# Last two heads' output products by token halves, with half of the routed layer's norm inside the attention's list schedule

## The chip, the cores and the metric

The kernel runs on one core of one Trainium2 chip. The metric is the device time of one execution in microseconds (us), the median of several runs. Positions in the text, such as "at 1092.9", are us from the start of the profiled execution's span.

## The reference, cut to what matters

512 tokens (4 sequences of 128) of width 2048 go through three residual layers: a small attention with a gated MLP, a 4-bit attention, and a routed layer. The change touches the end of the second and the beginning of the third.

```python
# 4-bit attention, added to x
w = (qw.astype(float32) - 8) * repeat(scales, 128, axis=0)     # _dequant_matmul: x @ w
q, k, v = (dequant_matmul(layernorm(x), w) for w in (q, k, v)) # 32 heads, 8 key heads, 128 wide
ctx = softmax(rope(q) @ rope(k).T / sqrt(128) + causal) @ v    # within each sequence
x = x + dequant_matmul(ctx, qw_o, scales_o)                    # the output product
# routed layer, added to x
h = layernorm(x)                                               # over the 2048 features of a token
base = h @ base_w.T + base_b
comb = top-2 of softmax(h @ router_w.T), normalised            # 16 experts
x = x + base + 0.5 * einsum(comb, h @ A.T, B)
```

The layer norm of a token needs all 2048 features of that token, so it can start only when every head's output product for that token has been added. It needs nothing of the other tokens.

## The kernel before

The residual x lives in SBUF as `R`, 16 feature tiles of 128 partitions by 512 tokens. The normed input of a layer lives as a pair `Nh`, `Nl` (a high and a low part, both in the reduced fp32r format of TensorE).

**The 4-bit attention.** There are 48 projections `u` (for each of 8 groups: key, value, 4 queries), each of 16 blocks, and 32 output products `h`, each of 16 blocks. A block (`Stream.block`, L1596) is two matmuls, high part (L1605) and low part (L1606), into a PSUM bank of 512 columns with tag `u` (6 of them), and an eviction that multiplies by the block's scale and adds. The eviction has two forms: `take_d` (L1614), one VectorE instruction that adds to `R` in place, or `take_p`, a ScalarE copy with a scale (L1624) followed by a GpSimd addition (L1628). The 4-bit weights come as int32 in three DMAs a head (`Stream.load`, L1581; 4 buffers `wi`), and ScalarE converts them (L1585; 6 buffers `wq`). Between projection and output product stands `attend` (L1719): scores (L1727, L1729), a maximum on VectorE (L1733), four exponentials and four divisions on ScalarE (L1739, L1750), a transpose (L1755), a copy (L1759), the product with the values (L1764), and the split of the result into `oh` (ScalarE, L1768) and `ol` (VectorE, L1771). These use two PSUM banks with tag `a`.

**What sets the order.** This whole stage is a list schedule: `op(engine, kind, emit, rank, needs, takes, gives)` records an operation, and `Plan.run` (L235) plays all engines through with the times of `Plan.TIME`. Whenever an engine is free it takes the ready operation with the lowest rank whose buffer (`takes`) has room, and emits it. The instruction order of TensorE, VectorE, ScalarE and GpSimd is then fixed as emitted, and on the chip each engine works through its list in order. Projection `u` has ranks from about `u` to `u + 1.8`. The output product of head `h`, which is query `i` of group `g` with `u = 6g + 2 + i`, has ranks from `u + 4.3 + 0.5 i`, over 1.5. For head 31 that is 52.8 to 54.3, and for head 30 it is 51.3 to 52.8. The choice between `take_d` and `take_p` is made in `Plan.run` by which engine comes free sooner.

**The routed layer** is recorded by another planner, `Deferred`, and ordered by `Deferred.solve` (L487): rank is the place in the program minus a shift from the table `RANKS`. It begins with the norm, one sequence `b` at a time: `Norm.enter(b)` transposes `R` back to tokens by features (4 PSUM tiles of 4 transposes each), takes statistics on VectorE, a root on GpSimd, and scales three tiles on ScalarE and one on VectorE. `Norm.leave(b)` transposes back (16 transposes) and splits into `Nh` (ScalarE) and `Nl` (VectorE). In program order: enter 0, 1; leave 0, 1; enter 2, 3; `low(halves[0])`, the router's and A's product for the first 256 tokens; the base product of two feature tiles for these tokens; leave 2, 3; and so on. All its instructions show as L485, the helper that issues them. Its SBUF and PSUM pools are opened after those of the attention are closed, so its tiles lie where the attention's did. The weights for `low` and for the first half of base tile 0 (`first_w`) are loaded and split during the attention.

Of the kernel before, what the change touches and what calls it, by code (L numbers as in the profile page):

```python
# [23 lines left out]
P = 128  # L24
B, S = 4, 128
T = B * S
# [35 lines left out]
K0 = 2  # L62
EARLY, EARLY_D = 2, ((1, 2), (1, 4), (1, 5), (1, 7))
# [3 lines left out]
    "add_x6": -277, "add_x7": -367, "add_x8": -331, "add_x9": -323, "base0": 108, "base11": -220, "base12": 23,  # L67
    "base13": -477, "base14": 9, "base15": -96, "base16": 1, "base19": -5, "base2": -665, "base20": -64,
    "base22": 17, "base23": -26, "base24": -125, "base25": 45, "base26": 70, "base27": -436, "base28": 53,
    "base30": -225, "base31": -44, "base32": -3, "base34": 73, "base35": -163, "base4": 30, "base5": -455,  # L70
    "base6": 382, "base7": 131, "base8": 18, "base9": 30, "bn0": 447, "bn1": -286, "bn2": -65, "bn3": 123,
    "bn3_0": 172, "bn3_1": 24, "bn3_10": 16, "bn3_11": 8, "bn3_12": 26, "bn3_13": -9, "bn3_14": -5,
    "bn3_15": 10, "bn3_16": -26, "bn3_17": 65, "bn3_18": -473, "bn3_2": 80, "bn3_20": -38, "bn3_21": -229,
    "bn3_22": 31, "bn3_24": -14, "bn3_25": -9, "bn3_26": -60, "bn3_27": 33, "bn3_28": -94, "bn3_29": -26,
    "bn3_3": 19, "bn3_30": 3, "bn3_31": -12, "bn3_4": 122, "bn3_5": 44, "bn3_6": 166, "bn3_7": -66,
# [14 lines left out]
    "enter3_2": 27, "enter3_3": -448, "enter3_4": 1213, "enter3_5": 351, "enter3_6": 130, "enter3_7": 10,  # L90
    "enter4": -529, "enter5": -21, "enter6": -1, "enter8": -294, "enter9": -89, "finish0": 27, "finish11": -18,
    "finish12": -195, "finish15": -89, "finish3": -1, "finish4": -155, "finish5": -15, "finish6": -50,
    "finish7": -9, "finish8": 59, "finish9": -55, "gated0": 78, "gated1": -102, "gated10": 12, "gated11": 104,
    "gated12": -23, "gated13": 24, "gated14": -122, "gated15": 58, "gated16": 133, "gated17": 34, "gated18": 20,
    "gated19": 28, "gated2": 91, "gated20": 123, "gated21": 89, "gated22": 12, "gated23": 69, "gated24": -1,
    "gated25": 2, "gated26": 65, "gated27": -130, "gated28": -215, "gated29": 8, "gated3": -2576, "gated30": 37,
    "gated31": -244, "gated4": 14, "gated5": -11, "gated6": 11, "gated7": -387, "gated8": -12, "gated9": -38,
    "load_ctx0": 117, "load_ctx1": 1, "load_ctx10": 86, "load_ctx11": -315, "load_ctx12": 65, "load_ctx13": 82,
    "load_ctx15": -2, "load_ctx2": 188, "load_ctx3": 12, "load_ctx4": -124, "load_ctx5": 100, "load_ctx6": -142,
    "load_ctx7": 77, "load_ctx8": 36, "load_ctx9": -136, "load_od0": -210, "load_od1": -129, "load_od10": 37,  # L100
    "load_od11": 265, "load_od12": 230, "load_od13": -71, "load_od14": -376, "load_od15": 55, "load_od2": 310,
    "load_od3": -29, "load_od4": 144, "load_od5": 102, "load_od6": -3, "load_od7": -1075, "load_od8": 201,
    "load_od9": -35, "low0": 196, "low1": 169, "low10": 0, "low11": 8, "low12": -96, "low13": -16, "low14": 58,
    "low15": -43, "low2": -38, "low3": -191, "low3_0": -226, "low3_1": -103, "low4": -12, "low5": -243,
    "low6": -68, "low7": 25, "low8": 333, "low9": -49, "mix0": 184, "mix1": 68, "mix10": 36, "mix11": 40,
    "mix12": 436, "mix13": 37, "mix14": -678, "mix15": -4, "mix2": 177, "mix3": 117, "mix4": -213, "mix5": 170,
    "mix6": 195, "mix7": 104, "mix8": -107, "norm0": 567, "norm1": 890, "norm2": 861, "norm3": -2, "out0": -4,
    "out1": 43, "out2": -47, "out3": 90, "out_a0": -344, "out_a1": 133, "out_a2": 14, "out_a3": 8,
    "out_m0": -47, "out_m1": -193, "out_m10": -332, "out_m11": 138, "out_m12": 108, "out_m13": -908,
    "out_m14": -492, "out_m15": -264, "out_m2": 156, "out_m3": -122, "out_m4": -698, "out_m5": 6, "out_m6": 163,  # L110
    "out_m7": -70, "out_m8": -90, "out_m9": -162, "outer0": -203, "outer1": -4, "outer2": -226, "outer3": -108,
    "parts0": 40, "parts1": -22, "parts10": -390, "parts11": 82, "parts12": -109, "parts13": -475,
    "parts14": 58, "parts15": -549, "parts16": -213, "parts17": -28, "parts18": 3, "parts19": -1, "parts2": 54,
    "parts20": 124, "parts21": 110, "parts22": -46, "parts23": 106, "parts24": 110, "parts25": -157,
    "parts26": 148, "parts27": 191, "parts29": 129, "parts3": -21, "parts30": 67, "parts31": 24,
    "parts32": -100, "parts33": 109, "parts34": -11, "parts35": 422, "parts36": 135, "parts37": 158,
    "parts38": 231, "parts39": 152, "parts4": -1166, "parts40": -50, "parts41": -111, "parts42": 71,
    "parts43": 47, "parts44": 78, "parts45": 165, "parts46": -30, "parts47": -332, "parts48": 39, "parts49": 7,
    "parts5": -71, "parts50": 63, "parts51": 7, "parts52": -361, "parts53": -25, "parts54": 40, "parts55": 23,
    "parts56": 56, "parts57": -275, "parts58": 124, "parts59": 107, "parts6": 79, "parts60": -87, "parts61": 49,  # L120
    "parts62": 95, "parts63": 6, "parts64": 8, "parts65": 122, "parts66": -9, "parts67": 26, "parts68": -195,
    "parts69": -6, "parts7": 66, "parts70": 122, "parts71": 138, "parts72": -68, "parts8": -22, "parts9": -45,
    "pick0": -72, "product0": -3, "product1": 22, "product10": 17, "product11": -86, "product2": -7,
    "product3": 83, "product4": 72, "product5": 79, "product6": 56, "product7": 14, "product8": -71,
    "product9": -73, "rate0": 1, "rate1": 11, "rate2": 47, "rate3": 62, "rate4": 89, "rate5": -41, "rate6": 9,
    "rate7": -8, "root0": -54, "root1": 647, "root2": 37, "root2_0": 54, "root2_1": 97, "root2_2": 110,
    "root2_3": 180, "root2_4": 84, "root2_5": -74, "root2_6": 215, "root2_7": 79, "root2_8": -6,
    "root2_9": -291, "root3": 529, "root3_0": 16, "root3_1": 3, "root3_2": 171, "root3_3": -42, "root3_4": 293,
    "root3_5": 9, "rope0": -66, "rope1": -145, "rope2": -211, "rope3": -180, "rope4": 68, "rope5": 48,
    "rope6": -33, "rope7": -20, "route0": -78, "rows0": -15, "rows1": 103, "rows2": 129, "rows3": 59,  # L130
    "rows_a0": -25, "rows_a1": 125, "scores0": -314, "scores1": 133, "scores2": 7, "scores3": 165, "select0": 7,
    "select1": -13, "select2": 44, "select3": -1101, "select4": -80, "select5": -380, "select6": -709,
    "select7": -620, "silu0": -55, "silu1": -20, "silu10": -56, "silu11": -14, "silu12": 40, "silu13": 35,
    "silu14": 91, "silu15": 78, "silu2": -69, "silu3": 4, "silu4": 144, "silu5": 123, "silu6": 157,
    "silu7": 113, "silu8": 162, "silu9": 219, "soft0": 41, "soft1": 76, "soft10": 37, "soft11": 80,
    "soft12": 44, "soft13": 179, "soft14": 163, "soft15": 52, "soft2": 158, "soft3": 83, "soft4": 77,
    "soft5": 164, "soft6": 131, "soft7": 87, "soft8": 141, "soft9": 130, "split0": -29, "split1": -478,
    "split10": -19, "split11": -260, "split12": -267, "split13": -301, "split14": -894, "split15": -914,
    "split16": -92, "split17": 29, "split18": -105, "split19": -485, "split2": -74, "split3": -10,
    "split3_0": -208, "split3_1": 29, "split3_10": -8, "split3_11": 13, "split3_14": 11, "split3_15": 70,  # L140
    "split3_16": 12, "split3_17": 55, "split3_18": 1, "split3_19": -10, "split3_2": 93, "split3_20": 201,
    "split3_22": -8, "split3_23": -12, "split3_24": 116, "split3_25": 41, "split3_26": 28, "split3_27": 21,
    "split3_29": 3, "split3_3": -15, "split3_30": 2, "split3_31": -2, "split3_32": 6, "split3_33": 15,
    "split3_34": 210, "split3_35": 32, "split3_36": -2, "split3_37": 6, "split3_38": 116, "split3_39": -20,
    "split3_40": -18, "split3_41": -54, "split3_5": -1, "split3_6": -29, "split3_7": 48, "split3_8": 13,
# [1984 lines left out]
```

## Time and profile before

| what | us |
|---|---|
| median of 3 runs (1413.06 to 1416.96) | 1414.34 |
| the profiled execution | 1413.73 |
| its span | 1411.9 |
| TensorE busy in the span | 1349.8 |
| VectorE / ScalarE / GpSimd busy | 1069.2 / 892.2 / 851.3 |
| last matmul of the attention starts | 1103.20 |
| GpSimd's last addition to `R` ends | 1105.82 |
| first matmul of the routed layer's base product starts | 1118.27 |
| last wait of the chain: VectorE's output instruction starts | 1408.00 |

The span is the time between the first and the last record; the execution is 1.8 us longer. TensorE is the busiest engine by far, at 96% of the span. Matmuls are pipelined, so a matmul's own record (0.39 us for 512 columns) is longer than the distance from one to the next (0.23 us), and the distance is what counts for the time.

### The profile page before, as it was taken

The numbers are of one execution on the slowest core, as the hardware profiler recorded it, in microseconds if no ns is written. First come the engines' busy times: TensorE is split into PE (matmuls) and PEld (weight loads), VectorE is DVE, ScalarE is ACT, GpSimd is POOL, SyncE is SP. The second block draws the span as 40 slices with busy tenths as digits, with TensorE's granted clock in tenths as the row PEclk, the third lists the DMA queues.
The fourth block names the chain that finished last, engine by engine and source line by source line (L and its number), as shares of the span: only waits on it lengthen the run. The fifth ranks groups of instructions, "written<-read, shape, count | busy, mean of one in ns | idle before, by whom it ended". The sixth has DMA issues, their size and how long they took to land.

```text
span 1411.9 us, 21943 instructions
## 1 busy us (share of the span) xinstructions
PE 1349.8 (96%) x7604; PEld 1144.6 (81%) x7604; DVE 1069.2 (76%) x1615; ACT 892.2 (63%) x1734; POOL 851.3 (60%) x700
## 2 busy tenths in 40 slices
PE   4999899999979999999999999999999899999998
PEld 4967898899966888888888888888887798888887
DVE  6886995797978999999999999999998734322221
ACT  5867555556776878878888787888888532211120
POOL 7782253262368798998989999898999302000000
PEclk9999999999999999999999999999999899999999
DMA  6120014655536354444444444444442112433331
GB/s 217 46 68 1 1 61 147 186 169 171 180 116 181 110 156 129 135 141 143 145 134 145 137 141 146 133 142 138 129 142 92 60 60 75 149 105 111 113 105 45
DMA packets 66983, 169.64 MB, mean 120 GB/s; under 512 B 9656, under 2 KB 11832, under 8 KB 66872
## 3 DMA queue, kind: packets, MB, share of 16 engines
q1 hardware_dynamic: 66872, 168.24, 38.2%
q8 instruction: 60, 0.98, 0.3%
q14 instruction: 51, 0.42, 0.1%
HBM read 153.53 MB, written 4.19 MB: 112 GB/s over the span
## 4 chain that ended last, share of the span: by engine, by line
PE 70%; DMA 4%; DVE 4%; ACT 3%; POOL 2%; issue 1%; SPq 0%; ACTq 0%; DVEq 0%; POOLq 0%
PE ps_q L485 21%; PE ps_u L1605 20%; PE ps_u L1606 19%; PE ps_p L485 4%; PE ps_a L1764 2%; PE ps_a L1729 2%; DMA st<-in_w_ctx 2%; DVE W L485 1%; DMA wi<-in_w_h 1%; PE ps_a L1755 1%; ACT W L485 1%; POOL acc L1628 1%; DMA st<-in_w_od_m 1%; DMA st<-in_xf 1%; PE acc L485 1%
## 5 line engine op out<-in xcount | busy, mean ns | idle before, releaser
L1614 DVE SCALAR_TENSOR_TENSOR acc<-ps_u,s_h,acc 128x512 f32<-128x512 f32 x506 | 376.9, 746 | 29.8 <-PE ps_u L1606 4.2
L1605 PE MATMUL ps_u<-Nh,wq 128*128 128x512 f32 (+1 forms) x768 | 305.5, 399 | 5.9 <-ACT wq L1585 2.6
L1606 PE MATMUL ps_u<-Nl,wq 128*128 128x512 f32 (+1 forms) x768 | 299.5, 391 | 0.0
L1628 POOL TENSOR_TENSOR R<-R,scaled 128x512 f32<-128x512 f32 x195 | 253.2, 1308 | 25.5 <-ACT scaled L1624 24.8
L1628 POOL TENSOR_TENSOR acc<-acc,scaled 128x512 f32<-128x512 f32 x184 | 240.1, 1305 | 27.6 <-ACT scaled L1624 26.0
L1614 DVE SCALAR_TENSOR_TENSOR R<-ps_u,s_o,R 128x512 f32<-128x512 f32 x317 | 230.6, 745 | 18.7 <-PE ps_u L1606 14.8
L1605 PE MATMUL ps_u<-oh,wq 128*128 128x512 f32 x512 | 209.0, 408 | 1.1 <-ACT oh L1768 0.7
L1606 PE MATMUL ps_u<-ol,wq 128*128 128x512 f32 x512 | 203.3, 397 | 0.9 <-DVE ol L1771 0.9
L1585 ACT ACTIVATE wq<-wi 128x640 fp32r<-128x640 int32 (+1 forms) x240 | 184.6, 770 | 23.2 <-PE ps_u L1606 18.8
L1605 PEld LDWEIGHTS ps_u<-Nh,wq 128*128 128x128 f32 x768 | 145.0, 189 | 46.3 <-ACT scaled L1624 8.5
L1606 PEld LDWEIGHTS ps_u<-Nl,wq 128*128 128x128 f32 x768 | 145.2, 189 | 30.3
L1624 ACT ACTIVATE scaled<-ps_u,s_o 128x512 f32<-128x512 f32 x195 | 132.8, 687 | 50.6 <-PE ps_u L1606 39.9
L485 ACT CAST w3h<-w 128x1024 fp32r<-128x1024 f32 x47 | 49.4, 1052 | 174.3 <-PE ps_q L485 152.6
L485 DVE TENSOR_TENSOR w3l<-w,w3h 128x1024 fp32r<-128x1024 f32 x47 | 57.5, 1223 | 122.6 <-ACT w3h L485 121.6
L1624 ACT ACTIVATE scaled<-ps_u,s_h 128x512 f32<-128x512 f32 (+1 forms) x188 | 127.2, 678 | 18.4 <-PE ps_u L1606 16.2
L1605 PEld LDWEIGHTS ps_u<-oh,wq 128*128 128x128 f32 x512 | 97.5, 190 | 25.6 <-ACT scaled L1624 3.5
L1606 PEld LDWEIGHTS ps_u<-ol,wq 128*128 128x128 f32 x512 | 97.4, 190 | 21.3 <-DVE ol L1771 1.7
L485 PE MATMUL ps_q<-Nh,w3l 128*128 128x512 f32 (+1 forms) x272 | 102.5, 377 | 0.0
L485 PE MATMUL ps_q<-Nh,w3h 128*128 128x512 f32 (+1 forms) x272 | 102.2, 376 | 0.0
L485 PE MATMUL ps_q<-Nl,w3h 128*128 128x512 f32 (+1 forms) x272 | 102.1, 375 | 0.0
L485 PE MATMUL ps_p<-Y,W 128*128 128x256 f32 x768 | 97.2, 285 | 2.2 <-DVE W L485 1.7
L485 PEld LDWEIGHTS ps_p<-Y,W 128*128 128x128 f32 x768 | 93.6, 191 | 3.4 <-DVE W L485 2.4
(251 smaller groups left out, 2654.4 us busy)
## 6 DMA issues: line engine op xcount, KB each, us to landing
wi<-in_w_h SPq DMA_DIRECT2D x96, 320.0 KB, 3.4
wi<-in_w_o SPq DMA_DIRECT2D x64, 320.0 KB, 3.5
wi<-in_w_h SPq DMA_DIRECT2D x48, 384.0 KB, 3.2
st<-in_w_ctx SPq DMA_DIRECT2D x32, 512.0 KB, 3.6
w<-in_w_base SPq DMA_DIRECT2D x32, 512.0 KB, 3.5
wi<-in_w_o SPq DMA_DIRECT2D x32, 384.0 KB, 3.3
swap<-acc SPq DMA_DIRECT2D x78, 128.0 KB, 2.6
st<-in_w_od_m SPq DMA_DIRECT2D x16, 512.0 KB, 3.7
```

The lines of the kernel that those rows point to most:

```text
L485: getattr(getattr(self.nc, c.engine), c.name)(*c.args, **c.kwargs)
L1585: nc.scalar.activation(w[:, : n * P], box["wi"][:, : n * P], AF.Copy, bias=-8.0)
L1605: nc.tensor.matmul(pm, self.w[i], hi, start=True, stop=False)
L1606: nc.tensor.matmul(pm, self.w[i], lo, start=False, stop=True)
L1614: "v", "less" if part else "evict", lambda: nc.vector.scalar_tensor_tensor(acc(), box["pm"], s, acc(), ALU.mult, ALU.add),
L1624: nc.scalar.activation(t, box["pm"], AF.Copy, scale=s)
L1628: "g", part + "add", lambda: nc.gpsimd.tensor_tensor(acc(), acc(), box["t"], ALU.add),
L1729: nc.tensor.matmul(sc[:, bs], q[:, bs], k[:, bs], start=False, stop=(b == B - 1))
L1755: nc.tensor.transpose(tp[:, bs], box["s"][:, bs], ident)
L1764: nc.tensor.matmul(po[:, bs], vals[h // HEADS][:, bs], box["pt"][:, bs], start=True, stop=True)
```

## The change

For the last two heads (`HALVED = 2`: 30 and 31) the output product is issued in two halves of 256 tokens. The first halves keep their ranks. The second halves get ranks 56 and 56.5, and their weights are loaded and converted a second time; in the list schedule these loads wait for the end of head 31's attention (`after`). The norm of sequences 0 and 1 moves from the routed layer into the list schedule as `normed(b, ...)` with ranks 50 and 51, ready when the first halves of all heads are in `R` (`r_half[0]`). It takes its PSUM tiles from the attention's tags (two `a` and two `u` a sequence) and its SBUF tiles from the attention's `acc`, `qT` and `swap`. The routed layer then starts with enter 2, enter 3. Some 90 entries of `RANKS` are changed too; all are steps of the routed layer (names such as `base`, `bn3_16` and up, `split3_`, `finish`), and the numbering of `bn3_`, `enter3_`, `root3_` and `turn4_` there now starts at sequence 2.

```diff
+HALVED = 2
...
-        "values": (0.89, 1.1), "half": (0.233, 0.43), "less_v": (0.39, 0.58), ...
+        "values": (0.89, 1.1), "half": (0.233, 0.43), "pow": (0.7, 0.85), "less_v": (0.39, 0.58), ...
...
-            def __init__(self, src, order, rank, step):
+            def __init__(self, src, order, rank, step, after=()):
+                self.after = list(after)
...
-                got = op("S", "dma", load, rank - DMA_LEAD, takes="wi")
+                got = op("S", "dma", load, rank - DMA_LEAD, self.after, takes="wi")
...
-        def output(h, rank, ready):
-            st = Stream(io["w_o"][h], range(KT), rank, OUT_SPAN / KT)
+        def output(h, rank, ready, cols=ALL, after=()):
+            st = Stream(io["w_o"][h], range(KT), rank, OUT_SPAN / KT, after)
+            ends = r_last if cols == ALL else r_half[cols.start]
             for m in range(KT):
-                acc = lambda m=m: R[:, m, :]
+                acc = lambda m=m: R[:, m, cols]
                 s = s_o[:, h * KT + m : h * KT + m + 1]
-                how = take(acc, s)
+                before = [o for o in {id(o): o for o in (ends[m], r_last[m])}.values() if o]
                 last = st.block(
-                    m, rank + OUT_SPAN * (m + 0.5) / KT, lambda h=h: outs[h], [ready], how,
-                    [r_last[m]] if r_last[m] else [],
+                    m, rank + OUT_SPAN * (m + 0.5) / KT, lambda h=h: tuple(a[:, cols] for a in outs[h]), [ready],
+                    take(acc, s, "" if cols == ALL else "less"), before[:1], cols,
                 )
-                r_last[m] = last
-            plan.ops[plan.last_block].gives.append("oh")
+                ends[m] = last
+            if cols.stop == T:
+                plan.ops[plan.last_block].gives.append("oh")
+
+        r_half = {c: [None] * KT for c in (0, T // 2)}
+
+        def normed(b, rank, ready):
+            bs = slice(b * S, (b + 1) * S)
+            box, tok, z = {}, {}, {}
+            banks, places = ("a", "a", "u", "u"), (("acc", "acc", "acc", "swap"), ("qT", "qT", "qT", "swap"))[b]
+            def turn(t):
+                tok[t] = tp = (ps_a if banks[t] == "a" else ps_u)()
+                for c in range(C):
+                    nc.tensor.transpose(tp[:, c * P : (c + 1) * P], R[:, 4 * c + t, bs], ident)
+            def stat(t):
+                if t == 0:
+                    box["st"] = tiny.tile([P, HT, 6], F32, tag="stats", name="stats")
+                nc.vector.bn_stats(box["st"][:, t, :], tok[t])
+            def mean():
+                box["mv"] = mv = tiny.tile([P, 2], F32, tag="mv", name="mv")
+                nc.vector.bn_aggr(mv, box["st"].rearrange("p t s -> p (t s)"))
+            def root():
+                box["rs"] = rstd(tiny, box["mv"][:, 1:2])
+            def shift():
+                box["nm"] = nm = tiny.tile([P, 1], F32, tag="nmr", name="nmr")
+                nc.vector.scalar_tensor_tensor(nm, box["mv"][:, 0:1], -1.0, box["rs"], ALU.mult, ALU.mult)
+            def scale(t):
+                z[t] = tmp(places[t])
+                if t in ZD:
+                    nc.vector.tensor_scalar(z[t], tok[t], box["rs"], box["nm"], ALU.mult, ALU.add)
+                else:
+                    nc.scalar.activation(z[t], tok[t], AF.Identity, scale=box["rs"], bias=box["nm"])
+            def back(q):
+                tok[q] = tp = (ps_a if banks[q] == "a" else ps_u)()
+                for i in range(4):
+                    nc.tensor.transpose(tp[:, i * P : (i + 1) * P], z[i][:, q * P : (q + 1) * P], ident)
+            def high(q):
+                nc.scalar.copy(Nh[:, 4 * q : 4 * q + 4, bs], heads(tok[q]))
+            def low(q):
+                d = (slice(None), slice(4 * q, 4 * q + 4), bs)
+                nc.vector.tensor_tensor(Nl[d], heads(tok[q]), Nh[d].bitcast(F32), ALU.subtract)
+            last = None
+            for t in range(HT):
+                p = op("p", "turn", lambda t=t: turn(t), rank, ready, takes=banks[t])
+                last = op("v", "reduce", lambda t=t: stat(t), rank, [p] + ([last] if last else []))
+            last = op("v", "root", mean, rank, [last])
+            last = op("g", "pow", root, rank, [last])
+            last = op("v", "root", shift, rank, [last])
+            ups = [
+                op("v" if t in ZD else "s", "evict", lambda t=t: scale(t), rank, [last], takes=places[t], gives=[banks[t]])
+                for t in range(HT)
+            ]
+            for q in range(HT):
+                p = op(
+                    "p", "turn", lambda q=q: back(q), rank, ups, takes=banks[q],
+                    gives=list(places) if q == HT - 1 else [],
+                )
+                h = op("s", "copy", lambda q=q: high(q), rank, [p])
+                op("v", "low", lambda q=q: low(q), rank, [h], gives=[banks[q]])
...
-                output(h, u + OUT_AT + 0.5 * i, ready)
+                output(h, u + OUT_AT + 0.5 * i, ready, ALL if h < NH - HALVED else slice(0, T // 2))
                 done[h] = ready
+        for b in range(2):
+            normed(b, NU + 2.0 + b, r_half[0])
+        for h in range(NH - HALVED, NH):
+            output(h, NU + 8.0 + 0.5 * (h - NH + HALVED), done[h], slice(T // 2, T), [done[NH - 1]])
...
-        for b in (0, 1):
-            norm.enter(b)
-        for b in (0, 1):
-            norm.leave(b)
         for b in (2, 3):
             norm.enter(b)
         low(halves[0])
```

## Prediction, made before the changed kernel was run

> **What bounds the kernel now.** I read the table of stages around the seam first, in steps of 6 us. Columns: stage, its length, then busy us of PE, PEld, DVE, ACT and POOL, the granted clock, DMA share, GB/s.
>
> ```profile
> 1078.00:1084.00 6.00, 5.08 (x31) 4.25 (x30) 6.00 (x9) 4.73 (x10) 5.48 (x5) 1.00 0.18 64
> 1084.00:1090.00 6.00, 5.53 (x25) 4.15 (x23) 5.51 (x10) 5.21 (x15) 6.00 (x6) 1.00 0.00 0
> 1090.00:1096.00 6.00, 4.58 (x16) 3.29 (x17) 1.44 (x2) 1.81 (x4) 2.13 (x2) 0.70 0.01 3
> 1096.00:1102.00 6.00, 6.00 (x21) 4.81 (x20) 3.58 (x5) 2.82 (x5) 5.00 (x4) 0.73 0.00 0
> 1102.00:1108.00 6.00, 5.16 (x39) 4.44 (x38) 4.29 (x8) 1.38 (x2) 4.02 (x5) 1.00 0.18 61
> 1108.00:1114.00 6.00, 2.49 (x17) 2.17 (x16) 5.15 (x13) 3.52 (x6) 1.56 (x4) 0.91 0.29 115
> 1114.00:1120.00 6.00, 6.00 (x41) 5.59 (x40) 5.26 (x10) 4.76 (x9) 0.00 (x0) 0.81 0.00 0
> ```
>
> Before 1090 four engines are nearly full. Then the clock falls to 0.70 and 0.73, and from 1108 to 1114 PE has 2.49 us of work in 6. The chain of waits says why (start, us, what):
>
> ```profile
> 1090.44 0.59 ACT softT L1759
> 1091.08 1.17 PE ps_a L1764 x8
> 1092.27 0.59 ACT oh L1768
> 1092.91 0.80 PE ps_u L1605
> ...
> 1105.86 3.09 DVE stats L485 x5
> ...
> 1110.48 1.45 ACT scaled L485 x2
> 1111.97 296.00 PE ps_q L485 x1475
> ```
>
> Head 31's softmax ends the first gap, the norm's chain (statistics, root, scale) the second, and from 1112 on PE is the chain to the end. So any us that PE starts its steady work earlier is a us of the span. The timeline of PE gives the two ends:
>
> ```profile
> 1104.42 3.71 PE L485 MATMUL ps_q<-ident,R 128*128 128x128 f32 x32 [0.84 <-ACT scaled L1624]
> 1111.31 0.33 PE L485 MATMUL ps_q<-ident,scaled 128*128 128x128 f32 x1 [3.17 <-ACT scaled L485]
> ```
>
> The steady stream begins at 1118.27 (first base matmul). By then 72 of the norm's 128 transposes are done, at 3.71 / 32 = 0.116 us each.
>
> What the seam loses, against full speed: head 31's wait 1088.74 to 1092.91 holds 4 transposes and 8 value products (0.44 + 0.9), so 2.8 us are lost; 32 matmuls from 1092.91 to 1103.43 would take 32 x 0.2275 = 7.3, so the clock costs 3.2; 1.0 until 1104.42; and 13.85 us hold 72 x 0.11 = 7.9 of transposes, so 5.9. Sum 12.9 us. That is all this change can win.
>
> **The change, part by part.** All times in the profiled execution (1413.73; the span is 1411.9; the median, 1414.34, lies 0.6 above it).
>
> *Head 30's second half leaves the cover of head 31's softmax.* Its 32 matmuls fill PE from 1081.59 to 1088.74. As halves they cost 0.119 us each (distance of 256-column matmuls at 418.90 to 419.14), so 32 take 3.8 us and PE runs dry at 1085.3 instead of 1088.7. In exchange head 31's softmax gets shorter. Its exponentials start at 1082.77, 1083.69, 1084.60 and 1085.95 because ScalarE puts a 0.58 us eviction after each, and the reciprocal waits 1 us behind VectorE's evictions. The half forms, from the first heads' half projections:
>
> ```profile
> 422.31 6.17 DVE L1614 SCALAR_TENSOR_TENSOR first_sum<-ps_u,s_h,first_sum 128x256 f32<-128x256 f32 x12 [0.84 <-PE ps_u L1606]
> 418.16 0.83 ACT L1624 ACTIVATE scaled<-ps_u,s_h 128x256 f32<-128x256 f32 x2
> 418.70 2.37 POOL L1628 TENSOR_TENSOR first_sum<-first_sum,scaled 128x256 f32<-128x256 f32 x3 [6.99 <-ACT scaled L1624]
> ```
>
> 0.83 for two on ACT is 0.48 + 0.35; so an eviction between two links costs 0.35, not 0.58. Six such places save 1.4, the gap before the fourth exponential 0.4, the reciprocal some 0.7: 2.5 us. `oh` then ends at 1090.3 instead of 1092.86. Bounds: 1092.9 (nothing saved) and 1088.5 (the links alone, after the scores' end at 1080.4: 0.68 + 4 x 0.35 + 0.2 + 4 x 0.35 + 0.4 + 0.58 + 0.9 + 0.58, and some 2 us for semaphores and for `ol` of head 30 ahead on VectorE). I take 1090.3. PE's gap grows from 1088.7-1092.9 to 1085.3-1090.3: 0.8 us longer, while the end comes 2.5 earlier.
>
> *First halves of head 31.* 32 x 0.119 = 3.8 us at full clock. After the gap before, the clock was low from about 1092.5 to 1099.3, with matmuls 0.43 us apart instead of 0.23. The new gap is longer, so I count 5 us of half clock, of which 2.4 are lost: 1090.3 + 6.2 = 1096.5. Bounds 1094.1 (no loss) and 1097.9 (all low).
>
> The Trainium skill ("TensorE: Matmul & The Clock Gate", Part 1: The HAM clock gate) says that a window of some 3.4 us without work halves the clock and that some 3.4 us of work restore it; the row above took 6.4 us to be restored. By the rule the first halves would lose 1.7 us instead of 2.4.
>
> *The second set of loads and conversions.* Six loads (four of 320 KB, two of 384), 2 MB more on 169.64; SP has nothing to issue between 1076.35 and 1105.85. On the chip the added dependence is only an order in the list, so these loads can go as soon as `wi` buffers are free, about 1077 to 1080; even if they waited for `ol` they would land 3.5 us later (median of the `in_w_o` rows), within the 6 us of the first halves. I count 0 on the path; without that cover 2 us. The conversions (0.73 each, L1585) are ScalarE's, below.
>
> *The norm beside the second halves.* From 1096.5 these engines have:
> - PE: 64 half matmuls, 7.6, and 64 transposes, 7.0: 14.6.
> - ACT: some 4 remaining conversions 2.9, 6 scalings x 0.67, 8 `Nh` copies x 0.53, that is 11.2, and 0.35 for each of `a` evictions.
> - DVE: 8 statistics x 0.62, 8 `Nl` x 0.62, 2 scalings x 0.75, 0.6 of small ones, that is 12.1, and 0.41 (a 1.66 us row of four at 405.17) for each of the other 32 - `a`.
> - POOL: 0.7 for each of `a`, and 1.6 for two roots.
>
> With `a` = 18: ACT 17.5, DVE 17.8, POOL 14.2. So this stage is bound by ACT and DVE, not by PE, and ends no sooner than 1096.5 + 17.6 = 1114.1. The chain inside gives nearly the same: `R` complete in its first half at 1097.5; statistics, root and scale of sequence 0 as in the rows 1105.86 to 1111.2, some 6 us; but both sequences want the two `a` banks, so sequence 1's first two tiles wait for sequence 0's scaling and then hold the banks that sequence 0's first two back-transposes need. Turn 0.5, statistics 3, root 1.5, scale 2.5 for each, and 3 to copy out: 15 to 16 us, 1113. I take 1114.5 for the last addition to `R`.
>
> *The routed layer's start.* Its first transposes read the second half of `R`, so PE starts at 1114.5 (before: 1104.42, with 64 more transposes to do). Then there are 32 transposes and 24 base matmuls (2.9 us, weights at hand) while sequence 2's chain runs, so the 5.9 us hole does not come back; I count 0.4 for what stays. Its weight loads start after the last addition, as at 1105.85; they need about 6 us until split, and PE has 3.7 + 2.9 us by then.
>
> **Sum.** Before, PE was at "64 transposes done, steady" at 1118.27 - 8 x 0.11 = 1117.4. Now 1114.5 + 0.4 = 1114.9. Gain 2.5 us: 1411.2 in the profiled execution, 1411.8 against the median. The seam's 12.9 us become 10.4: the hole at the norm is filled, but the gap before head 31 stays, the low clock stays, and the eviction engines need 3 us longer than PE.
>
> **Rivals.**
> 1. *The cover is as good as meant.* Head 31's chain ends at 1089, the clock is back after one short stretch, so the first halves end at 1093.5, and the planner packs the stage in 16.5 us with 2 more us of it laid beside the first halves: start at 1108 to 1112, 5.5 to 9.5 us gained, some 1407. For it: the chain's links alone give 1088.5. Against it: DVE and ACT were over 90% busy before 1090, and neither packs better than that.
> 2. *It moves the loss only.* Nothing is saved on head 31's chain (1092.9), and all else as above: 2.6 us later, 1414.3. For it: VectorE is full from 1078 to 1084, and the order there is the planner's, not the chip's.
> 3. *The clock stays low through the mixed stage, slower.* Transposes that wait for scalings are sparse work: the same kind of work from 1108 to 1120 ran at 0.91 and 0.81. PE's 14.6 us hide 3 us under ACT and DVE; every us at half clock beyond that costs half a us of stage. Low for all of it, PE needs 29.2 us, 11.6 more than 17.6, so 1423; low for four fifths of its time, 14.6 / 0.6 = 24.3, so 1418.5. It decides from 17.6 us of stage plus 2.5 of gain: slower than before once PE needs over 20.1, that is with 11 us of its time at half clock. Against it: half of PE's time there is dense matmuls.
>
> The Trainium skill ("TensorE: Matmul & The Clock Gate", Part 4: PE-mode transpose) says that transposes do not count as busy for the clock, which speaks against a stage with 64 of them. The 32 at 1104.42 ran 0.116 apart at clock 1.00, so here they at least did not lose it at once. By the rule the time would be rival 3's.
>
> **Chances.** A measurement of this kernel can tell 0.3%, 4.2 us. The forecast has 0.49, between 1409 and 1414.3 (bounds of `oh` and of the clock, each 2 us, partly offsetting); 0.06 of it lies under 1410.1 and counts as faster. Rival 1 has 0.28, all faster; rival 2 0.11, the same; rival 3 0.12, of which 0.09 are slower by over 0.3% and 0.03 lie within it. So faster 0.34, same 0.57, slower 0.09. The range leaves out the far ends of rivals 1 and 3, together under 0.2: 1405.5 to 1417.0.
>
> **What would show it.** In the profile after: PE's gap before head 31's first half matmul begins near 1085 and ends near 1090; half matmuls 0.21 apart for some 5 us; statistics of the norm between 1097 and 1106 with evictions among them; DVE and ACT over 90% busy to 1114; the routed layer's first transposes near 1114.5 and no hole of 3 us after them. The forecast is wrong if that start is before 1112 or after 1118.

## The result, and the profile after

| | before | after |
|---|---|---|
| median of 22 runs each, us | 1413.78 (1409.12 to 1417.64) | 1419.41 (1414.65 to 1425.14) |
| profiled execution / its span | 1413.73 / 1411.9 | 1420.66 / 1418.8 |
| head 31's `oh` ends | 1092.85 | 1091.23 |
| last addition to `R` ends | 1105.83 | 1119.44 |
| first matmul of the routed layer's base product | 1118.27 | 1124.88 |

The changed kernel is **slower**, by 0.4%: the ratio of after to before is 1.0041, 95% interval 1.0030 to 1.0053, or 5.8 us (4.2 to 7.5). The forecast was 2.5 us faster, with a range that ended at 1417.0.

The stages of the changed kernel, in the columns of the prediction's table:

```profile
1090.00:1096.00 6.00, 5.18 (x23) 4.60 (x22) 2.63 (x5) 2.34 (x5) 2.09 (x3) 0.51 0.01 3
1096.00:1102.00 6.00, 5.46 (x44) 5.26 (x43) 5.02 (x12) 5.12 (x11) 4.95 (x8) 0.93 0.30 94
1102.00:1108.00 6.00, 4.04 (x28) 3.43 (x27) 3.96 (x10) 3.49 (x7) 3.08 (x6) 0.93 0.08 28
1108.00:1114.00 6.00, 5.36 (x32) 4.88 (x32) 4.94 (x9) 4.57 (x10) 2.08 (x4) 0.79 0.00 0
1114.00:1120.00 6.00, 5.29 (x36) 4.17 (x35) 5.57 (x13) 4.17 (x9) 3.70 (x7) 1.00 0.01 3
```

The mixed stage, from 1098 to 1123, is not full on any engine as a whole: VectorE (the third busy number) is busy for 20.9 of the 25 us, PE for 19.4, ScalarE for 18.3. VectorE comes near only from 1114 to 1120 (5.57 of 6); between 1102 and 1108 it is at 3.96 and ScalarE at 3.49. That no engine fills the stage speaks for a chain in it, and against a bound by one engine's work; the experiments test this.

The chain of waits, and PE's timeline (start, busy us, instruction, count; in brackets the idle time before and what ended it):

```profile
1123.11 0.04 issue
1123.16 291.56 PE ps_q L488 x1444
```

```profile
1091.29 0.58 PE L1609 MATMUL ps_u<-oh,wq 128*128 128x256 f32 x1 [0.68 <-ACT oh L1772]
...
1100.66 1.04 PE L1819 MATMUL ps_a<-ident,R 128*128 128x128 f32 x8
1101.54 1.91 PE L1819 MATMUL ps_u<-ident,R 128*128 128x128 f32 x16
...
1108.43 1.05 PE L1819 MATMUL ps_a<-ident,R 128*128 128x128 f32 x4
...
1109.71 1.01 PE L1819 MATMUL ps_a<-ident,R 128*128 128x128 f32 x4
...
1123.16 1.97 PE L488 MATMUL ps_q<-ident,R 128*128 128x128 f32 x16 [1.74 <-DVE Nl L1854]
```

Once PE is in the routed layer it is the chain to the end, as before. What let it start is not an addition to `R`, the last of which had ended at 1119.44, but the last `Nl` of the moved norm, at 1123.10. These first matmuls read only `R` and write a PSUM tile of the routed layer; so it isn't the value of `Nl` that they wait for but, as the code has it, the place of the tiles that the norm still reads. The norm's first transposes take six tiles at 1100.66 and 1101.54. The last two tiles, sequence 1's `a` tiles, come 7.8 and 9.1 us later.

Within the norm, the instructions stand in line behind evictions. VectorE, then GpSimd:

```profile
1104.12 0.25 DVE L1828 BATCH_NORM_AGGREGATE mv<-stats 128x2 f32<-128x24 f32 x1
1105.37 0.48 DVE L1618 SCALAR_TENSOR_TENSOR R<-ps_u,s_o,R 128x256 f32<-128x256 f32 x1 [0.99 <-PE ps_u L1610]
1106.87 0.48 DVE L1618 SCALAR_TENSOR_TENSOR R<-ps_u,s_o,R 128x256 f32<-128x256 f32 x1 [1.02 <-PE ps_u L1610]
1107.27 0.15 DVE L1835 SCALAR_TENSOR_TENSOR nmr<-mv,rstd 128x1 f32<-128x1 f32 x1
```

```profile
1104.91 0.73 POOL L1632 TENSOR_TENSOR R<-R,scaled 128x256 f32<-128x256 f32 x1 [2.67 <-ACT scaled L1628]
1105.61 0.22 POOL L662 TENSOR_SCALAR rstd<-mv 128x1 f32<-128x1 f32 x1
1105.92 0.57 POOL L663 TENSOR_TENSOR rstd<-rstd,minus_half 128x1 f32<-128x1 f32 x1
```

The variance is ready at 1104.37, but GpSimd's root starts at 1105.61, behind an addition that waited for ScalarE. The root ends at 1106.49, but `nmr` starts at 1107.27, behind an eviction that waited 1.02 us for a matmul. That is 1.2 + 0.8 us in the chain at whose end the routed layer starts.

**A measure without the noise of the early part.** Head 30's output product starts at 1074.4 to 1081.6 in the profiled executions below, though the work before it is nearly the same; the early part varies from execution to execution. So I count from its first matmul to the start of VectorE's last output instruction. From base tile 0's first matmul on, this takes 289.7 to 290.6 us in each whole kernel; nearly all differences lie in the seam. The last column is the time at half clock between 9 and 51 us on this count, from the granted clock of the trace.

| kernel (us from head 30's first output matmul) | `oh` of 31 ends | routed layer's first matmul | base tile 0 | whole | ratio of times to before, 95% interval | half clock, us |
|---|---|---|---|---|---|---|
| before | 12.66 | 24.23 | 38.08 | 327.81 | | 10.2 |
| after | 11.89 | 43.82 | 45.54 | 335.40 | 1.0041 (1.0030 to 1.0053) | 10.2 |
| e3: halves only | 11.64 | 27.82 | 40.92 | 330.71 | 1.0021 (1.0007 to 1.0035) | 6.8 |
| e9: norm moved only | 12.65 | 42.86 | 44.58 | 334.64 | 1.0037 (1.0024 to 1.0051) | 13.7 |
| e10: e9, other banks | 12.64 | 39.29 | 41.01 | 330.97 | 1.0025 (1.0009 to 1.0042) | 6.8 |
| e1: after, other banks | 11.58 | 42.08 | 43.81 | 333.69 | 1.0028 (1.0014 to 1.0043) | 10.2 |
| e4: one head halved | 12.64 | 42.17 | 43.86 | 333.75 | 1.0037 (1.0021 to 1.0052) | 10.2 |
| e5: e4, other banks | 12.64 | 37.97 | 40.76 | 330.63 | 1.0029 (1.0011 to 1.0047) | 10.2 |
| e2: loads held back | 11.81 | 40.94 | 42.64 | 332.53 | 1.0035 (1.0019 to 1.0052) | 6.8 |
| e6: fewer on VectorE | 11.44 | 44.36 | 47.02 | 337.58 | 1.0060 (1.0035 to 1.0084) | 13.7 |
| e7: no second halves | 11.09 | 36.81 | 38.54 | (work left out) | | 10.2 |
| e8: e7, other banks | 11.09 | 35.07 | 38.15 | (work left out) | | 17.1 |

In before and e3 the routed layer's first matmul begins the norm of sequences 0 and 1; in the others that norm is done by then, and it is sequence 2's. So base tile 0 is the column to compare.

These are single executions, and the clock makes them differ. Half clock comes in steps of 3.4 us, and not alike where the work is alike: e7 and e8 both end `oh` at 11.09, but behind it e7 has one step and e8 two, and the norm's first transposes come at 17.18 and 18.12. A step holds 1.7 us of work at full clock, so it can cost up to 1.7 us where PE is what is waited for. A difference of that size in this table may be the execution's and not the kernel's. The ratios of times, over 5 to 22 executions of each kernel, are the check on it.

### The profile page after: what moved, and what is told of

Read it like the earlier page. It is cut to its first block, busy times and chain, and to the rows that moved or that the text cites. A ratio compares the mean times of both kernels' runs of the same rounds, so it can differ in the third digit from the quotient of the medians.

```text
span 1418.8 us, 22149 instructions
## 1 busy us (share of the span) xinstructions
PE 1353.9 (95%) x7668; PEld 1150.1 (81%) x7668; DVE 1071.5 (76%) x1634; ACT 898.5 (63%) x1753; POOL 852.0 (60%) x713
## 5 line engine op out<-in xcount | busy, mean ns | idle before, releaser
L1632 POOL TENSOR_TENSOR R<-R,scaled 128x512 f32<-128x512 f32 (+1 forms) x208 | 253.9, 1231 | 34.8 <-ACT scaled L1628 33.5
L1618 DVE SCALAR_TENSOR_TENSOR R<-ps_u,s_o,R 128x512 f32<-128x512 f32 (+1 forms) x336 | 234.5, 716 | 19.8 <-PE ps_u L1610 15.1
L1609 PE MATMUL ps_u<-oh,wq 128*128 128x512 f32 (+1 forms) x544 | 215.6, 399 | 5.5 <-ACT scaled L1628 2.6
L1610 PE MATMUL ps_u<-ol,wq 128*128 128x512 f32 (+1 forms) x544 | 207.8, 384 | 1.2 <-DVE ol L1775 1.0
L1589 ACT ACTIVATE wq<-wi 128x640 fp32r<-128x640 int32 (+1 forms) x246 | 189.2, 770 | 22.2 <-PE ps_u L1610 18.4
L1628 ACT ACTIVATE scaled<-ps_u,s_o 128x512 f32<-128x512 f32 (+1 forms) x208 | 135.7, 660 | 49.7 <-PE ps_u L1610 39.7
L1609 PEld LDWEIGHTS ps_u<-oh,wq 128*128 128x128 f32 x544 | 104.4, 192 | 31.4 <-ACT scaled L1628 7.9
L1610 PEld LDWEIGHTS ps_u<-ol,wq 128*128 128x128 f32 x544 | 104.6, 192 | 19.6 <-DVE ol L1775 1.7
```

The costliest lines, as they stand in the source:

```text
L1589: nc.scalar.activation(w[:, : n * P], box["wi"][:, : n * P], AF.Copy, bias=-8.0)
L1609: nc.tensor.matmul(pm, self.w[i], hi, start=True, stop=False)
L1610: nc.tensor.matmul(pm, self.w[i], lo, start=False, stop=True)
L1618: "v", "less" if part else "evict", lambda: nc.vector.scalar_tensor_tensor(acc(), box["pm"], s, acc(), ALU.mult, ALU.add),
L1628: nc.scalar.activation(t, box["pm"], AF.Copy, scale=s)
L1632: "g", part + "add", lambda: nc.gpsimd.tensor_tensor(acc(), acc(), box["t"], ALU.add),
```

## The experiments

**The theories.** A: the moved norm is a chain in which sequence 1 gets its two `a` banks only when sequence 0 has scaled, and sequence 0's way back only when sequence 1 has scaled; nothing of the routed layer lies beside it. B: the work is the bound, on VectorE and ScalarE, or the second loads. C: the evictions that stand ahead of the norm's instructions in the fixed orders.

**e3, halves only.** The norm stays in the routed layer, and `RANKS` is that of before.

```diff
-        for b in range(2):
-            normed(b, NU + 2.0 + b, r_half[0])
...
+        for b in (0, 1):
+            norm.enter(b)
+        for b in (0, 1):
+            norm.leave(b)
```

> Edit: only the token halves of the output products; the norm of sequences 0 and 1 is back in the routed layer, with the ranks of before. This is the cost of halving by itself. If the longer gap ahead of head 31 (4.5 us of PE idle instead of 1.9) and the conversions cost what the trace of after shows: measure 327.8 + 3 to 4 = 331 to 332. If halving is free: 327.8. So under theory A the moved norm costs 3 to 5 us more than it hides; under rival B halving accounts for most of the 7.6.

Measured 330.71, just under the 331 to 332 of a halving that isn't free. PE's timeline, at the routed layer:

```profile
1106.24 3.68 PE L486 MATMUL ps_q<-ident,R 128*128 128x128 f32 x32 [0.98 <-DVE R L1616]
1112.43 0.33 PE L486 MATMUL ps_q<-ident,scaled 128*128 128x128 f32 x1 [2.51 <-ACT scaled L486]
```

The hole behind the first 32 transposes is there as in before (2.51 us instead of 3.17). Head 31's `oh` is 1.0 us earlier, but head 30's second halves now come after its softmax and not beside it, and the half evictions there stand in a row (19 on VectorE in 8.18 us, 0.43 each, where a whole one took 0.68). `R` is complete 2.9 us later (28.52 instead of 25.64). Halving the products alone costs 2.9 us here, with one step of half clock less than before; by the times it is 3.0 (1.0 to 4.9).

**e9, the norm moved and nothing halved.**

```diff
-HALVED = 2
+HALVED = 0
...
-            normed(b, NU + 2.0 + b, r_half[0])
+            normed(b, NU + 2.0 + b, list(r_last))
```

> No token halves: heads 30 and 31 whole, as before, and only the norm of sequences 0 and 1 moved into the list schedule, ready when all of R is. Measured from head 30's first output matmul, as in the other runs. Theory A (the moved norm is a chain with two a banks that nothing hides, since nothing of the routed layer can lie beside it): head 31's `oh` at 12.7 and the first transposes of R at 24.2 as before, then 19.6 us of chain as in the run without second halves: the routed layer's first matmul at 43.9, base tile 0 at 45.6, the whole 335.3 (before 327.8), a ratio near 1.005. Rival B (VectorE and ScalarE bound the stage through the evictions of the second halves): there are none here, so the norm takes the 13.85 us that it took in the routed layer: base tile 0 near 40 to 41, the whole 330.

Measured 334.64, near A's 335.3; B's 330 is missed by 4.6. By the times the move costs 5.2 us (3.4 to 7.2). The parts are less near: the first transposes came at 22.1, not 24.2, and from there it took 20.8 us, not 19.6. With no second halves in the way, PE's timeline shows the bank exchange by itself:

```profile
1096.43 0.49 PE L1819 MATMUL ps_a<-ident,R 128*128 128x128 f32 x3
...
1098.91 1.91 PE L1819 MATMUL ps_u<-ident,R 128*128 128x128 f32 x16
1103.54 1.42 PE L1819 MATMUL ps_a<-ident,R 128*128 128x128 f32 x8 [2.71 <-ACT acc L1842]
...
1110.91 0.90 PE L1847 MATMUL ps_a<-ident,acc 128*128 128x128 f32 x3 [4.25 <-ACT qT L1842]
...
1117.23 1.97 PE L488 MATMUL ps_q<-ident,R 128*128 128x128 f32 x16 [1.56 <-DVE Nl L1854]
```

PE waits 2.71 us until sequence 0's scaling (`acc`) has freed the `a` tiles, and 4.25 us until sequence 1's scaling (`qT`) has freed them again. Two chains that could run side by side run one after the other. From 1104.6 to 1114.9 the clock is at half as well.

**e10, as e9, and sequence 1 takes four `u` banks.**

```diff
-            banks, places = ("a", "a", "u", "u"), (("acc", "acc", "acc", "swap"), ("qT", "qT", "qT", "swap"))[b]
+            banks, places = (("a", "a", "u", "u"), ("u", "u", "u", "u"))[b], (("acc", "acc", "acc", "swap"), ("qT", "qT", "qT", "swap"))[b]
```

> As the run with only the norm moved, and sequence 1 takes all its PSUM tiles from the u banks. Theory A: the chain is 16.9 us as in the run without second halves with these banks, so the routed layer's first matmul at 41.1, base tile 0 at 42.9, the whole 332.6; 2.7 less than with the a banks. Rival B: the banks do nothing, 330 as in the other run.

Measured 330.97: 3.7 us less than e9, where A said 2.7 and B nothing. But e9's norm had three steps of half clock and e10's one. PE worked for some 6.0 us of them in e9 and 3.4 in e10, so up to 1.3 of the 3.7 may be the clock's. By the times the two differ by 1.7, within the noise.

```profile
1101.29 2.78 PE L1819 MATMUL ps_u<-ident,R 128*128 128x128 f32 x24
1107.03 0.33 PE L1847 MATMUL ps_a<-ident,acc 128*128 128x128 f32 x1 [2.96 <-ACT acc L1842]
...
1116.25 1.97 PE L488 MATMUL ps_q<-ident,R 128*128 128x128 f32 x16 [1.89 <-DVE Nl L1854]
```

All 32 transposes now go at once, and both long waits become one of 2.96. Still 3.2 us above before. There the same chain had 16 transposes of sequences 2 and 3 in its waits, and base tile 0 started with 8 transposes of sequence 1 still to come; here the routed layer's first matmul waits for the norm's last `Nl`, and 16 transposes more come before base tile 0.

**e7 and e8, the norm with the first halves alone**, with the banks of after (e7) and of e10 (e8). The second token halves of heads 30 and 31 are left out.

```diff
-        for h in range(NH - HALVED, NH):
+        for h in ():
```

> Leaves out: the second token halves of the output products of heads 30 and 31, with their loads (rows of the output for sequences 2 and 3 miss them). So the moved norm has the engines to itself. Chain from its first transposes to its last Nl, 22.4 us after the change. Theory A: 18 to 20, since the wait for the two a banks is inside it. Rival C (sharing the engines with the second halves): 13 to 15, as the routed layer's own norm took 13.9 to the first base matmul before.

> Leaves out the same as the run before, and sequence 1 takes its four PSUM tiles from tag u. Theory A: 13 to 15 us, 4 to 5 less than with the two a banks. Rival C: the same as with the two a banks, within 1 us.

From the norm's first transposes to the routed layer's first matmul, e7 takes 36.81 - 17.18 = 19.6 us (A right, C's 13 to 15 not met), e8 35.07 - 18.12 = 16.9 (A too low by 2 to 4). In after it is 22.5. So of these 22.5, 2.9 come from sharing the engines with the second halves and 2.7 from the two banks, both against the clock: the norm has one step of half clock in after, two in e7 and three in e8. The waits of e7:

```profile
1104.83 1.33 PE L1819 MATMUL ps_a<-ident,R 128*128 128x128 f32 x8 [2.71 <-ACT acc L1842]
...
1111.58 0.90 PE L1847 MATMUL ps_a<-ident,acc 128*128 128x128 f32 x3 [4.54 <-ACT qT L1842]
```

They are e9's, to 0.3 us.

**e1, after with the banks of e10** (the same edit).

> Edit: in the moved norm, sequence 1 takes all four of its PSUM tiles from tag u instead of two from a. Measure: from head 30's first output matmul to the last output instruction; 327.8 us before, 335.4 after the change. Theory A (the two a banks: sequence 1's first two tiles wait for sequence 0's scaling and then hold the banks that sequence 0's first two back-transposes need, so the norm's chain of 22.4 us ends last): the chain falls to 14 to 16 us, the routed layer starts 5 to 7 us earlier, measure 329 to 331. Rival B (the stage is bound by the work of ScalarE and VectorE, as I predicted, or by the late start): the same work remains, measure 334 to 336.

The norm's chain fell from 22.4 to 16.0 us, as A said. The total fell by 1.7 only (A's 329 to 331 is missed by 3 to 5), with the same time at half clock:

```profile
1107.60 0.55 PE L1609 MATMUL ps_u<-oh,wq 128*128 128x256 f32 x1 [3.10 <-DVE acc L1840]
...
1121.72 1.97 PE L488 MATMUL ps_q<-ident,R 128*128 128x128 f32 x16 [1.22 <-DVE R L1618]
```

The norm now holds all six `u` banks, so the second halves stand still for 3.10 us, and at the end the routed layer waits for an addition to `R` instead of `Nl`. The banks are needed by both; freeing one delays the other.

**e4, only head 31 halved** (`HALVED = 1`), and **e5, with the banks of e10**.

> Edit: HALVED = 1, so only head 31 is halved, head 30's whole product covers head 31's softmax as before, and three loads are repeated instead of six. Theory A: the norm's chain is as long as after the change (20 to 23 us from its first transposes), and only the gap ahead of head 31 goes, so measure 332 to 334. Rival B (work of the eviction engines): 16 fewer half evictions on their path, 6 to 7 us less, 328 to 329.

> Edit: HALVED = 1 and sequence 1's four PSUM tiles from tag u. With HALVED = 1 alone the routed layer's first transposes came 42.2 us after head 30's first output matmul, 12 us after the last addition to R, so the norm's chain (19.6 us) was all that was waited for. Theory A (banks): the chain falls to the 16 us that it took with these banks, the routed layer starts at 38 to 39, measure 329.5 to 330.5 (before: 327.8). Rival C (not the banks, but order and contention): the chain stays at 19 to 20, measure 333 to 334.

e4's stages (3 us each) show the norm with nearly nothing beside it:

```profile
1109.00:1112.00 3.00, 1.02 (x10) 0.78 (x8) 3.00 (x6) 1.18 (x3) 0.00 (x0) 1.00 0.00 0
1112.00:1115.00 3.00, 0.41 (x3) 0.41 (x4) 1.51 (x4) 1.24 (x2) 0.79 (x2) 0.98 0.00 0
1115.00:1118.00 3.00, 3.00 (x16) 2.81 (x15) 1.46 (x3) 2.53 (x5) 0.00 (x0) 0.50 0.00 0
```

`R` is complete at 29.97, 10 us sooner than in after, and base tile 0 is only 1.7 us sooner: 333.75, as A said and not as B. With the other banks it is 330.63, again near A, with the same time at half clock in all. From 1112 to 1115 PE has 0.41 us of work, and then its clock is 0.50.

**e2, the second loads held back** until head 31's `ol` is made, by a small GpSimd write that the list schedule orders after it.

```diff
...
-                got = op("S", "dma", load, rank - DMA_LEAD, self.after, takes="wi")
+                def hold():
+                    box["wi"] = gw.tile([P, 6 * P], I32, tag="wi", name="wi", bufs=4)
+                    nc.gpsimd.memset(box["wi"][:, :1], 0)
+                first = [op("g", "root", hold, rank - DMA_LEAD, self.after, takes="wi")] if self.after else []
+                got = op("S", "dma", load, rank - DMA_LEAD, first, takes=None if first else "wi")
```

> Edit: GpSimd writes one column into each buffer of the six repeated loads after head 31's attention (in the list's order), so that the loads can't be issued before. Rival B (the repeated loads are issued at 1075.9, right behind the routed layer's first weight load, share the DMA with it, and ScalarE's cast of that weight then stands in front of head 31's exponentials): the cast comes 1.6 us earlier, the first half product of head 31 starts 1.6 us earlier, measure 333.5 to 334. If the loads don't matter: no change, 335.4. Theory A says nothing of the loads; its chain of 22 us from the first transposes stays.

In after ScalarE waited 1.79 us for a base weight, behind the second loads, just ahead of head 31's exponentials. After first, then e2:

```profile
1080.86 1.05 ACT L1903 CAST fh<-w 128x1024 fp32r<-128x1024 f32 x1 [1.79 <-DMA w<-in_w_base]
1081.82 0.46 ACT L1628 ACTIVATE scaled<-ps_u,s_o 128x256 f32<-128x256 f32 x1
1082.19 0.35 ACT L1743 ACTIVATE soft<-ps_a,nm 128x128 f32<-128x128 f32 x1
```

```profile
1079.67 1.05 ACT L1909 CAST fh<-w 128x1024 fp32r<-128x1024 f32 x1
1081.77 0.47 ACT L1634 ACTIVATE scaled<-ps_u,s_o 128x256 f32<-128x256 f32 x1 [1.05 <-PE ps_u L1616]
```

The wait for the load is gone, and the eviction behind it now waits 1.05 us for head 30's first low product instead. Counted from head 30, the first exponential comes 0.6 us sooner (2.23 instead of 2.85), but then the value product runs at half clock for its whole length (1.89 us instead of 1.36), and `oh` ends at 11.81 instead of 11.89. So the loads cost 0.6 us at the exponentials, and in this execution the clock took most of it back. The whole is 332.53, 2.9 us shorter all the same, and below both values expected. The order in the mixed stage is another one: counted from head 30, the first transposes of `R` come 1.5 us earlier and sequence 0's `nmr` 2.5 earlier. That is C's kind of gain, had by chance; e2 also has no half clock in that stage, where after has one step, and one execution can't part the two.

**e6, 10 of the 32 second-half blocks to VectorE instead of about 18.**

```diff
-                    take(acc, s, "" if cols == ALL else "less"), before[:1], cols,
+                    take(acc, s, "" if cols == ALL else "less") if cols.start == 0 else (take_d if m % 3 == 1 else take_p)(acc, s, "less"),
+                    before[:1], cols,
```

> Edit: the second halves' evictions are divided by feature tile, 10 of 32 to VectorE and 22 to ScalarE with GpSimd, instead of by the planner's choice (some 18 to VectorE). From the first transposes to the routed layer took 22.5 us after the change. If VectorE's work bounds that stage (12.1 us of norm and 0.41 for each eviction): 8 evictions less are 3.3 us less, measure 332 to 332.5. If the wait for the two a banks bounds it (theory A): within 1 us of 335.4.

Slower by 2.2 than after. The routed layer's first matmul comes 0.5 us later, still behind an `Nl`, as A said; `R` is complete at 44.66 instead of 40.10, by then on ScalarE and GpSimd's way. The other 1.6 us come after the start, where this execution had a step of half clock: the first transposes take 2.7 us to base tile 0 instead of 1.7, and the rest 290.6 instead of 289.9. With some 8 evictions less on VectorE the stage wasn't shorter, so VectorE's load was not what held it.

**What stands.** Moving the norm costs 6.8 us by itself, halving the products 2.9; both cost 7.6, so laying the one beside the other gives back 2.1 of 9.7. By the times the three are 5.2, 3.0 and 5.8: the same picture, but with intervals of 2 us to either side it isn't shown that the overlap gives back anything. That the moved norm is a loss by itself is clear of the noise (e9's interval, 1.0024 to 1.0051). The two `a` banks cost time in all four pairs: 3.7 (e9 to e10, of which up to 1.3 may be the clock's), 1.7 (after to e1) and 3.1 (e4 to e5) at the same half clock in all, and 2.7 of the chain (e7 to e8, with the clock against it). How much they cost in general stays open; by the times the three pairs give 1.1 to 1.8, each within the noise. With other banks the parts cost 3.2 and 2.9 and together 5.9 (e1): there the overlap gives back nothing that could be told. C is read off the timelines and agrees with e2, but no run took those evictions away alone. That a part of the routed layer could lie beside the moved norm, if its tiles didn't wait for the attention's, wasn't tried. No version here beats the kernel before.

## Why the prediction was wrong, step by step

Counted from head 30's first matmul the forecast put the routed layer's start at 1114.9 - 1080.2 = 34.7; it came at 43.8. The 9.1 us lie in three steps, and 1.0 more comes after.

- **Head 31's softmax: 1.8 us late.** `oh` was to end at 10.1 and ended at 11.9, so 0.8 of the 2.5 us was saved. Between the first and the fourth exponential 0.63 us went (3.18 to 2.55), near the 0.7 of three shorter evictions, but the 0.4 counted for the gap before the fourth stayed. The first one started 0.27 later (2.85 from head 30's first matmul instead of 2.58), behind a cast that waited 1.79 us for its load, beside the second loads. In e7, which has no second loads, it started at 2.24. So the second loads, counted as 0 on the path, cost some 0.6. From the fourth on only 0.42 was saved where 1.4 was counted; the value product took 1.36 us at low clock instead of 1.17. The step took all of the idle time on ScalarE as saved; its order has other waits in it. In e7 `oh` ends at 11.1, so 1.0 of the 1.8 is there without the second loads too.
- **First halves: 0.5 late.** 6.7 us instead of 6.2. The low clock lasted from 1091.3 to 1096.7, near the 5 us that were counted, and there is a wait of 0.4 for `ol`.
- **The mixed stage: 6.8 late, the step that failed.** It took 25.2 us (1097.96 to 1123.16) instead of 18.4. The bound by work, 17.6, didn't decide (and VectorE's work was 20.9, not 17.8). The norm's first transposes came 2.7 us after the first halves' last matmul, where 1.0 was counted: the last addition of a first half ended 1.8 after it, and 16 matmuls of the second halves stood ahead in PE's order. The chain, put at 15 to 16 us, took 22.4: 3.2 for sequence 0's transposes and statistics, 3.6 to `nmr` (1.5 counted), 1.0 to sequence 1's first `a` tile, 5.4 for its statistics (3.5 counted), 2.9 to its `nmr` (1.5 counted), 2.2 to scale, 4.2 to copy out (3 counted). The prediction named the two banks and the exchange, and then priced the chain by its links alone, as if no eviction stood ahead of them. It also added them up wrong: 7.5 for each sequence and 3 are 18, not 15 to 16, so some 2.5 us are the sum's own and 4.4 the links'. And it let the routed layer wait for the last addition to `R` (1119.44); what ended last was the last `Nl`, 3.7 us later.
- **After the start: 1.0.** PE has no hole there, as forecast. But base tile 0 starts with 48 transposes to do instead of 56, and the rest takes 289.86 us against 289.73; the 0.9 for eight transposes isn't gained, and the profile shows no wait of PE that would say why. This stays open.

Right were the length of PE's gap (4.7 us, 1086.6 to 1091.3, where 5.0 was forecast), the early issue of the loads, and no hole after the routed layer's start. The gap's place was not: both its ends came some 2 us late on the count from head 30, since the half products ahead of it took 5.9 us from the first low product on and not 3.8, with waits for evictions between them. So its length is in part luck. Rival 1 falls: head 31's chain gained 0.8 us, not 4. Rival 2 is nearer (softmax nearly unsaved), but kept the stage as forecast. Rival 3 had the sign, and by luck nearly the size (1418.5), and not the cause: the clock is low again from 1107.4 to 1111, but PE waits between, and its work never fills the stage.

Part of what was missing needs no run, though no size follows from it: before, 13.85 us lead from the norm's first transposes to base tile 0, with 16 transposes of other sequences in its waits. The moved norm lost these and got 64 half matmuls, which need its banks, in their place; and it must be done to its last `Nl` before the routed layer's first matmul, where before base tile 0 started within it.

## What to carry to other kernels

Price a moved chain by its links in the order in which each engine will issue them, with the instructions that stand ahead of each link, and not by the work per engine: where every engine has idle time, the sum of work is only a lower bound. Count the buffers that two chains share; two chains on one pair of banks run one after the other, and giving one of them more banks takes them from the work that was to cover it. Price the two halves of a change apart: here the halves cost 2.9 (e3) and the move 6.8 (e9), and the overlap had to win 9.7 us to break even. And look at the granted clock before reading a small difference between two profiles.

## What the runs showed of the hardware

Transposes alone can bring the clock back. In e9, from 1110.91 on, PE does nothing but transposes, 0.21 us apart; from 1115.07 on they are 0.11 apart, some 4 us later. The Trainium skill ("TensorE: Matmul & The Clock Gate", Part 4: PE-mode transpose) says that the full clock doesn't engage for transposes, since they don't count as busy in the same way. Here it did, and the measurement decides. In e7 the same work from 1111.58 to 1117 stayed at half clock (0.50 from 1112 to 1115, 0.57 from 1115 to 1118), so 4 us aren't always enough.

Around the seam, half clock came in steps of 3.4 us in all these traces. Behind head 31's wait it lasted 6.8 us in seven of the twelve profiled executions (before and after among them) and 3.4 in the other five. The prediction had counted 5 for the changed kernel.
